# Last batch of a mixture of experts: where the second bias is added, and how the combined sums are turned

## The chip, the cores and the metric

The kernel runs on one core of a Trainium2 chip. The metric is the time of one execution in microseconds, measured on the device; lower is better. The kernel before takes 3936.42 us, the median of three runs (3930.62 to 3939.96).

## What is computed

The input x is 4 images of 384 channels and 32 x 32 points. Layer 0 is a group normalisation, a selective scan over the points in four directions (16 states per channel), a layer norm and a gelu, added to x. Layer 1 takes the points as tokens (4 batches of 1024 tokens of 384 numbers) and adds windowed attention and then a mixture of experts. The change lies in the mixture's end:

```python
scores = jnp.einsum('bsd,de->bse', x, gate_w) + gate_b
probs = jax.nn.softmax(scores, axis=-1)
topk_vals, topk_idx = jax.lax.top_k(probs, TOP_K)          # 2 of 4 experts
mask = jnp.sum(jax.nn.one_hot(topk_idx, NUM_EXPERTS, dtype=probs.dtype), axis=-2)
masked = probs * mask
masked = masked / (jnp.sum(masked, axis=-1, keepdims=True) + 1e-09)
h = jax.nn.gelu(jnp.einsum('bsd,edh->ebsh', x, w1) + b1[:, None, None, :], approximate=False)
y = jnp.einsum('ebsh,ehd->ebsd', h, w2) + b2[:, None, None, :]
out = jnp.einsum('bse,ebsd->bsd', masked, y)
```

All is in 32-bit floats. The bias b2 of an expert is added to each of its outputs, and the two chosen outputs of a token are then weighted with their gates and summed.

## The kernel before

**A recording layer sets the order.** The kernel is written as generators that yield operations. A small planner (`Machine`, lines 218 to 382) keeps a clock for each engine, an assumed cost for each operation and the assumed times at which tiles are written and read, and records on each engine the operation that it holds to be ready first; the numbers EARLY, LATER and the like are handicaps. What is recorded is a fixed program: each engine executes its own list in that order and waits on semaphores. So the order of all later work depends on every assumed time. Buffers come from stocks (`Stock`, line 78): `take` waits until one is free, `give` hands it back together with the later of its assumed writing and reading times (line 113). SP issues all plain DMAs, POOL the indirect ones.

**The scan.** Its 768 steps, in blocks of 128 rows by 1024 points, run over batch after batch. For each step POOL multiplies (`times_b`), ACT makes the decay dA (`decay`), DVE scans, POOL or DVE multiplies by c, and PE folds pairs of steps (`fold_y`). When it has ended (line 879 and on), two more PSUM banks and 15 more row tiles are handed to the other stages: the stock `rows` then has 25.

**Tokens and routes.** When a batch's scan is done, `tokens(b)` runs its 8 tiles of 128 tokens through attention; `route(n)` then sorts half a batch (4 tiles) into blocks of at most 128 tokens of one expert and scatters the tokens' rows into xsdr. A batch has 5 blocks from its first half and 14 from its second, 19 in all and 76 in the kernel.

**A block of an expert.** `loads` (line 1369) reads the block's expert number e and its row rw into registers of SP, and loads b1, the tokens xb and eight pieces of 576 KB of the weights w1 and w2 (w_sb, eight buffers). `turn_in` transposes the tokens, `hidden` makes four groups of nine matmuls (ps_hid), `gelus` the activation, `output` twelve matmuls into one PSUM tile y_ff. `leave` (line 1438) copies y_ff to the one SBUF tile yb and stores it to ysdr. When all 19 blocks of a batch have left, the batch counts as done (line 1447).

**The combination.** `combine(b)` (line 1449) has a generator `one(a)` for each of a batch's 8 tiles. It loads o, the residual, turned (channels on partitions); transposes the gates p of the four experts into a row tile gt (ps_gt); gathers the two expert outputs of each token into gs[0] and gs[1] from ysdr; and weights and sums them, ACT into the PSUM tile ps_c and DVE into gs[0]. Six matmuls into ps_c follow: three with the identity, which turn the sums, and three of b2_sb with gt, which add the gated second bias. DVE adds o, and SP stores the result. For the last batch all 8 tiles run at once and take o and gt early, when their half has been routed; their gathers wait for the batch's last block. The rows gt and gs are given back after the matmuls are recorded (lines 1488 and 1489).

Of the kernel before, what the change touches and what calls it, by code (L numbers as in the profile page):

```python
# [13 lines left out]
ALU = mybir.AluOpType  # L14
# [3 lines left out]
P = 128  # L18
B, D, HH, WW = 4, 384, 32, 32
L = HH * WW  # L20
T = D // P
# [13 lines left out]
NE, HID = 4, 4 * D  # L35
# [357 lines left out]
def conv_attn_hybrid(  # L393
# [11 lines left out]
    def const_load(src, shape, name):  # L405
        dst = const.tile(shape, F32, name=name)
        nc.sync.dma_start(dst, src)
        return dst
# [12 lines left out]
    b2_sb = const_load(b2, [NE, D], "b2_sb")  # L421

    ident = const.tile([P, P], F32, name="ident")
# [64 lines left out]
    banks = Stock(m, ps_b, "ps", 4, [P, HB])  # L488
# [3 lines left out]
    with tc.tile_pool(name="setup", bufs=1) as setup:  # L492
# [16 lines left out]
        for j in range(JB):  # L509
            ps = banks.now("ps_al")  # L510
# [22 lines left out]
    rows = Stock(m, work, "row", NROW, [P, D])  # L533
# [21 lines left out]
    ysdr = [dram.tile([(SPARE + 1) * P, D], F32, name="ysdr", tag=f"ys{n}", bufs=1) for n in range(2)]  # L555
# [16 lines left out]
    pe, act, dve, pool, sp = m.pe, m.act, m.dve, m.pool, m.sp  # L572
# [8 lines left out]
    def copy(dst, src):  # L581

        if on_vector():
            yield from dve.tensor_copy(dst, src)
        else:
            yield from act.copy(dst, src)

    def on_vector():
        lead = FAVOUR if count_of["scan"] < NSLOT else 0.1
        return m.clock["dve"] + lead < m.clock["act"]  # L590
# [768 lines left out]
    rws, bbs, xts, w1s, w2s, hids, left = {}, {}, {}, {}, {}, {}, {}  # L1359

    def turn_in(i, xb):
        xt = yield from xbts.take("xbt")
        ps = yield from three("ps_xb", xb)
        yield from copy(xt[:, :D], ps[:, :D])
        banks.give(ps)
        xts[i] = xt
        xbs.give(xb)

    def loads():
        for i, (n, o) in enumerate(ffn):  # L1370
            yield lambda: n in routed
            xs, idx, p, eid, gate = routed[n]
            e = yield from sp.value_load(eid[0:1, 0, o : o + 1], min_val=0, max_val=NE - 1)
            rw = yield from sp.value_load(eid[0:1, 1, o : o + 1], min_val=0, max_val=SPARE * P)
            rws[i] = rw
            bb = yield from bbs_.take("bb")
            yield from sp.dma_start(bb.unsqueeze(1), b1[:, bass.ds(e, 1), :])
            bbs[i] = bb
            xb = yield from xbs.take("xb")
            yield from sp.dma_start(xb, xs[bass.ds(rw, P), :])  # L1380
            m.spawn(turn_in(i, xb), LATER)
            for store, src in ((w1s, wl1), (w2s, wl2)):
                for c in range(NCH):
                    w = yield from wts.take("w_sb")
                    yield from sp.dma_start(w, src[bass.ds(e, 1), c].rearrange("e p f -> p (e f)"))
                    store[i, c] = w
# [33 lines left out]
    def output():  # L1420
        for i in range(len(ffn)):
            for c in range(NCH):
                yield lambda: (i, c) in hids and (i, c) in w2s
            yield m.settled(*(hids[i, c] for c in range(NCH)))
            y = yield from banks.take("y_ff")
            for c in range(NCH):
                mm = Calls()
                for j in range(HT):
                    mm.matmul(
                        y[:, :D], hids[i, c][:, ts(j, P)], w2s[i, c][:, ts(j, D)],  # L1430
                        start=c == 0 and j == 0, stop=c == NCH - 1 and j == HT - 1,
                    )
                yield from pe.all(mm)
                wts.give(w2s.pop((i, c)))
                hss.give(hids.pop((i, c)))
            m.spawn(leave(i, y), LATER)

    def leave(i, y):
        b = PARTS[ffn[i][0]][0]
        yb = yield from ybs.take("yb")  # L1440
        yield from copy(yb[:, :D], y[:, :D])
        banks.give(y)
        yield from sp.dma_start(ysdr[b % 2][bass.ds(rws.pop(i), P), :], yb[:, :D])
        ybs.give(yb)
        left[b] = left.get(b, 0) + 1
        if left[b] == sum(SIZES):
            have.add(("experts", b))

    def combine(b):

        def one(a):
            n, a_in = 2 * b + a // PT, a % PT
            if b == B - 1:
                yield lambda: n in routed
            xs, idx, p, eid, gate = routed[n]
            if b == B - 1:
                o, gt = yield from rows.take("cb", n=2)
            else:
                o, gt, *gs = yield from rows.take("cb", n=4)
            yield from sp.dma_start(  # L1460
                o[:, :D].rearrange("p (t l) -> p t l", t=T), t2dr[b][:, :, ts(a, P)]
            )
            ps = yield from banks.take("ps_gt")
            yield from pe.transpose(ps[:NE, :P], p[:, a_in, :], ident)
            yield from copy(gt[:NE, :P], ps[:NE, :P])
            banks.give(ps)
            if b == B - 1:
                yield lambda: ("experts", b) in have
                gs = yield from rows.take("cb", n=2)
            for n in range(2):  # L1470
                yield from pool.indirect_dma_start(
                    out=gs[n][:, :D], out_offset=None, in_=ysdr[b % 2],
                    in_offset=bass.IndirectOffsetOnAxis(ap=idx[:, n, a_in : a_in + 1], axis=0),
                )
            yield m.settled(*gs)
            ps = yield from banks.take("ps_c")
            yield from act.activation(ps[:, :D], gs[0][:, :D], AF.Copy, scale=gate[:, 0, a_in : a_in + 1])
            yield from dve.scalar_tensor_tensor(
                gs[0][:, :D], gs[1][:, :D], gate[:, 1, a_in : a_in + 1], ps[:, :D], ALU.mult, ALU.add
            )  # L1480
            mm = Calls()
            for t in range(T):
                c = ts(t, P)
                mm.matmul(ps[:, c], gs[0][:, c], ident, start=t == 0, stop=False)
            for t in range(T):
                c = ts(t, P)
                mm.matmul(ps[:, c], b2_sb[:, c], gt[:NE, :P], start=False, stop=t == T - 1)
            yield from pe.all(mm)
            rows.give(gt, *gs)
            yield from dve.tensor_tensor(o[:, :D], ps[:, :D], o[:, :D], ALU.add)  # L1490
            banks.give(ps)
            yield from sp.dma_start(
                out[b].rearrange("(t p) h w -> p t (h w)", p=P)[:, :, ts(a, P)],
                o[:, :D].rearrange("p (t l) -> p t l", t=T),
            )
            rows.give(o)

        yield from m.together([one(a) for a in range(NT)], 2 if b < B - 1 else NT, LATER)
        have.add(("out", b))

# [16 lines left out]
    with tc.manual_schedule():  # L1517
        for b in range(B):
            m.spawn(group_norm(b), EARLY)
        for gen in (turn_loads(), time_steps(), state_rows(0), state_rows(1), spread(1), spread(0)):  # L1520
            m.spawn(gen, EARLY)
        for gen in (decay(), times_b(), scan()):
            m.spawn(gen)
        m.spawn(layer1(), EARLY)
        m.spawn(routes(), EARLY)
        for gen in (prepare(), loads(), hidden(), output(), mixture()):
            m.spawn(gen, LATER)
        m.run()
# [54 lines left out]
```

## Time and profile before

| what | us |
|---|---|
| median of three runs | 3936.42 |
| the profiled execution | 3933.02 |
| its span, from the first to the last instruction | 3931.3 |
| PE busy | 3031.9 |
| DVE busy | 2911.4 |
| POOL busy | 2879.7 |
| ACT busy | 2441.7 |

The profile is of one execution. "PE" stands for the matmuls of TensorE, "PEld" for its weight loads, DVE for VectorE, ACT for ScalarE, POOL for GpSimd and SP for SyncE, which here only issues DMAs. A line number such as L148 or L159 is that of the planner's helper that issues every operation, so tiles tell the work apart: `ps_c<-ident,cb` writes ps_c from the identity and a row tile. A 32-bit matmul leaves two records, a transpose one. Views used below are the page, the chain of waits that ended last, the timeline (instructions in order of time, equal neighbours merged), groups of instructions, and busy time by stage.

### The profile page before, as it was taken

How to read it: one execution, taken by the hardware profiler on the slowest of the kernel's cores; microseconds unless marked ns; L12 is line 12 of the kernel's file. 1: busy time of each engine (PE TensorE's matmuls, PEld its weight loads, DVE VectorE, ACT ScalarE, POOL GpSimd, SP SyncE). 2: the span in 40 equal slices, each digit the busy share in tenths (PEclk: the TensorE clock that was granted, in tenths of full speed). 3: DMA queues.
4: the chain of work that ended last, by engine and by line, in shares of the span. 5: the costliest groups of instructions: out<-in, count | busy, mean ns of one | idle time of the engine just before them, and what ended most of it. 6: DMA issues, size and time to landing. Idle time of an engine off the chain costs nothing. (4 is left out here: it accounts for less than half of the span.)

```text
span 3931.3 us, 50281 instructions
## 1 busy us (share of the span) xinstructions
PE 3031.9 (77%) x15880; PEld 1853.6 (47%) x15880; DVE 2911.4 (74%) x3331; ACT 2441.7 (62%) x4050; POOL 2879.7 (73%) x1498
## 2 busy tenths in 40 slices
PE   2555555588677898777687769888878999998997
PEld 1100010055444555434354536556545566877786
DVE  2999999988778788898887797877778884332001
ACT  2544454467787788866667858887677775542221
POOL 1999989988888887898898789888887994012001
PEclk8555566577789899977778879988888999998997
DMA  5776775534558998935377769865567997448995
GB/s 205 266 266 208 275 271 185 193 120 153 175 170 306 329 395 303 336 136 170 107 268 259 259 245 374 293 219 176 182 217 268 363 365 235 143 151 298 318 321 184
DMA packets 394147, 953.66 MB, mean 243 GB/s; under 512 B 49621, under 2 KB 173401, under 8 KB 393881
## 3 DMA queue, kind: packets, MB, share of 16 engines
q1 hardware_dynamic: 385688, 925.27, 67.2%
q0 software_dynamic: 8192, 25.17, 1.8%
q8 instruction: 126, 2.06, 0.2%
q14 instruction: 141, 1.15, 0.1%
HBM read 786.39 MB, written 182.78 MB: 247 GB/s over the span
## 5 line engine op out<-in xcount | busy, mean ns | idle before, releaser
L148 POOL TENSOR_TENSOR z<-dts,bc 128x1024 f32<-128x1024 f32 x768 | 1793.4, 2358 | 178.5 <-PE ps_y L159 93.6
L148 ACT ACTIVATE dA<-dts,a 128x1024 f32<-128x1024 f32 x768 | 851.7, 1116 | 473.7 <-DVE z L148 448.8
L159 PE MATMUL ps_y<-z,fold 128*32 128x512 f32 x3072 | 730.6, 771 | 487.7 <-POOL z L148 262.9
L148 POOL TENSOR_TENSOR z<-z,bc 128x1024 f32<-128x1024 f32 x383 | 898.2, 2356 | 139.7 <-DVE z L148 130.0
L148 DVE TENSOR_TENSOR_SCAN dA<-dA,z 128x1024 f32<-128x1024 f32 x385 | 880.6, 2287 | 135.5 <-ACT dA L148 128.5
L148 DVE TENSOR_TENSOR_SCAN z<-dA,z 128x1024 f32<-128x1024 f32 x383 | 862.3, 2276 | 57.0 <-ACT dA L148 54.5
L159 PEld LDWEIGHTS ps_hid<-xbt,w_sb 128*128 128x128 f32 x5472 | 674.4, 200 | 152.8 <-issue 50.7
L159 PE MATMUL ps_hid<-xbt,w_sb 128*128 128x128 f32 x5472 | 698.9, 286 | 48.8 <-DMA w_sb<-wl 13.1
L159 PE MATMUL y_ff<-w_sb,hs 128*128 128x384 f32 x1824 | 659.7, 503 | 28.8 <-ACT hs L148 17.8
L159 PEld LDWEIGHTS ps_y<-z,fold 128*32 128x32 f32 x3072 | 93.8, 120 | 915.3 <-POOL z L148 448.2
L148 DVE TENSOR_TENSOR z<-dA,bc 128x1024 f32<-128x1024 f32 x385 | 470.0, 1221 | 13.2 <-DVE dA L148 0.5
L148 ACT ACTIVATE hs<-ps_hid,bb 128x128 f32<-128x128 f32 x912 | 276.2, 368 | 306.3 <-PE ps_hid L159 255.4
L159 PEld LDWEIGHTS y_ff<-w_sb,hs 128*128 128x128 f32 x1824 | 333.7, 195 | 276.1 <-issue 58.4
L148 POOL DMA_INDIRECT cb<-ysdr,idx x64 | 62.6, 978 | 320.0 <-DMA ysdr<-yb 274.1
L148 ACT ACT_TABLE_LOAD x194 | 248.9, 1283 | 10.3 <-PE ps_g L159 3.6
L304 ACT ACT_TABLE_LOAD x194 | 248.9, 1283 | 4.1 <-PEq L1568 0.8
L159 POOL TENSOR_TENSOR rn<-rn,half 128x1 f32<-128x1 f32 x96 | 52.8, 550 | 212.2 <-DVE rn L159 203.2
L148 DVE COPY yb<-y_ff 128x384 f32<-128x384 f32 x24 | 13.4, 557 | 248.8 <-PE y_ff L159 233.3
L148 ACT ACTIVATE ed<-ps_dt,dtb_sb 128x512 f32<-128x512 f32 x192 | 125.4, 681 | 83.9 <-PE ps_dt L148 78.8
L148 POOL DMA_INDIRECT xsdr<-tks,idx x64 | 65.1, 1016 | 141.8 <-DVE idx L159 56.6
L148 PE MATMUL ps_dt<-xd,dtw_sb 12*128 12x512 f32 x192 | 135.6, 816 | 20.0 <-DMA dtw_sb<-in_dtw_dram 14.7
L148 DVE TENSOR_TENSOR ps_dt<-ps_dt,ed 128x512 f32<-128x512 f32 x192 | 132.7, 691 | 11.7 <-ACT ps_dt L148 8.8
(202 smaller groups left out, 3293.8 us busy)
## 6 DMA issues: line engine op xcount, KB each, us to landing
w_sb<-wl SPq DMA_DIRECT2D x608, 576.0 KB
dts<-dtr SPq DMA_DIRECT2D x384, 512.0 KB
bc<-xdr SPq DMA_DIRECT2D x128, 512.0 KB
dtr<-ed SPq DMA_DIRECT2D x192, 256.0 KB
ub<-udr SPq DMA_DIRECT2D x48, 512.0 KB
yp<-ydr SPq DMA_DIRECT2D x96, 256.0 KB
ydr<-yp SPq DMA_DIRECT2D x96, 256.0 KB
wl<-in_w_dram SPq DMA_DIRECT2D x32, 576.0 KB
```

The lines of the kernel that those rows point to most:

```text
L148: return getattr(self.real, op)(*a, **k)
L159: getattr(self.real, op)(*a, **k)
L304: self.nc.scalar.add_instruction(mybir.InstLoadActFuncSet(name=self.nc.get_next_instruction_name(), act_func_set_id=EXP_LN_SET,))
```

## The change

In the last batch alone, b2 is no longer added in the combination. `leave` loads the row of b2 that belongs to the block's expert into all 128 partitions of yb and adds y_ff to it on DVE, in place of the copy; for this, `loads` keeps the register e beside rw until the block leaves. In the combination of the last batch the row gt, the transpose of the gates and its copy are left out, and the sums are turned by three transposes instead of three matmuls with the identity. In the other batches these operations stay, and the row gt is given back before their six matmuls are recorded and not after.

```diff
             rw = yield from sp.value_load(eid[0:1, 1, o : o + 1], min_val=0, max_val=SPARE * P)
-            rws[i] = rw
+            rws[i] = e, rw
...
     def leave(i, y):
         b = PARTS[ffn[i][0]][0]
+        e, rw = rws.pop(i)
         yb = yield from ybs.take("yb")
-        yield from copy(yb[:, :D], y[:, :D])
+        if b == B - 1:
+            yield from sp.dma_start(
+                yb[:, :D], b2[bass.ds(e, 1), :].to_broadcast([P, D])
+            )
+            yield from dve.tensor_tensor(yb[:, :D], y[:, :D], yb[:, :D], ALU.add)
+        else:
+            yield from copy(yb[:, :D], y[:, :D])
         banks.give(y)
-        yield from sp.dma_start(ysdr[b % 2][bass.ds(rws.pop(i), P), :], yb[:, :D])
+        yield from sp.dma_start(ysdr[b % 2][bass.ds(rw, P), :], yb[:, :D])
...
             if b == B - 1:
-                o, gt = yield from rows.take("cb", n=2)
+                o = yield from rows.take("cb")
             else:
                 o, gt, *gs = yield from rows.take("cb", n=4)
...
-            ps = yield from banks.take("ps_gt")
-            yield from pe.transpose(ps[:NE, :P], p[:, a_in, :], ident)
-            yield from copy(gt[:NE, :P], ps[:NE, :P])
-            banks.give(ps)
-            if b == B - 1:
+            if b < B - 1:
+                ps = yield from banks.take("ps_gt")
+                yield from pe.transpose(ps[:NE, :P], p[:, a_in, :], ident)
+                yield from copy(gt[:NE, :P], ps[:NE, :P])
+                banks.give(ps)
+            else:
                 yield lambda: ("experts", b) in have
                 gs = yield from rows.take("cb", n=2)
...
             mm = Calls()
-            for t in range(T):
-                c = ts(t, P)
-                mm.matmul(ps[:, c], gs[0][:, c], ident, start=t == 0, stop=False)
-            for t in range(T):
-                c = ts(t, P)
-                mm.matmul(ps[:, c], b2_sb[:, c], gt[:NE, :P], start=False, stop=t == T - 1)
+            if b < B - 1:
+                for t in range(T):
+                    c = ts(t, P)
+                    mm.matmul(ps[:, c], gs[0][:, c], ident, start=t == 0, stop=False)
+                for t in range(T):
+                    c = ts(t, P)
+                    mm.matmul(ps[:, c], b2_sb[:, c], gt[:NE, :P], start=False, stop=t == T - 1)
+                rows.give(gt)
+            else:
+                for t in range(T):
+                    mm.transpose(ps[:, ts(t, P)], gs[0][:, ts(t, P)], ident)
             yield from pe.all(mm)
-            rows.give(gt, *gs)
+            rows.give(*gs)
```

## The prediction

> **What bounds the kernel now.** I read the page's busy table and its 40 slices, then the chain of waits, then the end in the timeline, and last the busy time by stage.
>
> ```profile
> PE 3031.9 (77%) x15880; PEld 1853.6 (47%) x15880; DVE 2911.4 (74%) x3331; ACT 2441.7 (62%) x4050; POOL 2879.7 (73%) x1498
> PE   2555555588677898777687769888878999998997
> DVE  2999999988778788898887797877778884332001
> POOL 1999989988888887898898789888887994012001
> ```
>
> Until slice 33 POOL and DVE, which carry the scan, are the fullest rows; from there PE stands at 9 and the other two fall. The last scan instruction starts at 3276 us. So there are a scan stretch and, from about 3280, one in which PE works off what is left of the mixture of experts.
>
> ```profile
> 3100.00:3200.00 100.00, 96.29 (x573) 63.62 (x573) 86.76 (x56) 73.53 (x111) 96.70 (x46) 0.99 1.02 392
> 3200.00:3300.00 100.00, 96.70 (x603) 66.91 (x602) 73.17 (x46) 72.38 (x111) 75.68 (x33) 1.00 0.86 294
> 3674.00:3690.00 16.00, 16.00 (x100) 12.93 (x99) 0.56 (x1) 3.90 (x13) 0.00 (x0) 1.00 0.94 317
> 3886.00:3932.00 46.00, 25.41 (x96) 21.63 (x96) 8.94 (x17) 4.67 (x8) 15.19 (x16) 0.54 0.37 107
> ```
>
> The columns are PE, PEld, DVE, ACT, POOL, granted clock, DMA share, GB/s. PE is already full in the last 180 us of scan; in the steady blocks of the last batch it has no gap (a block takes 16.1 us, the distance of two evictions of y_ff); at the end its clock is down to 0.54.
>
> ```profile
> 3895.73 3.04 DMA cb<-ysdr,idx
> 3899.56 12.70 PE ps_c L159 x48
> 3913.41 6.39 PE ps_c L159 x24
> 3921.05 6.36 PE ps_c L159 x24
> 3927.44 0.56 DVE cb L148
> ```
>
> The chain's end: after one gather has landed, eight tiles of ps_c on PE follow one another, 3.15 us each (two groups of three, below).
>
> ```profile
> 3888.77 0.99 POOL L148 DMA_INDIRECT cb<-ysdr,idx  x1 [274.05 <-DMA ysdr<-yb]
> 3891.96 0.97 POOL L148 DMA_INDIRECT cb<-ysdr,idx  x1 [2.20 <-issue]
> ...
> 3910.61 0.95 POOL L148 DMA_INDIRECT cb<-ysdr,idx  x1 [0.30 <-issue]
> ...
> 3924.18 1.65 PE L159 MATMUL ps_c<-ident,cb 128*128 128x128 f32 x6
> 3925.75 1.65 PE L159 MATMUL ps_c<-cb,b_sb 4*128 4x128 f32 x6
> ```
>
> The 16 gathers leave POOL every 1.25 us, the last at 3910.6; without PE's queue the end would stand some 4 us after that.
>
> ```profile
> 3609.62 0.99 POOL L148 DMA_INDIRECT xsdr<-tks,idx  x1 [1.94 <-DMA xsdr<-tks,idx]
> 3609.81 5.29 SPq L148 DMA_DIRECT2D cb<-t2dr  x8
> 3621.72 0.88 PE L159 MATMUL ps_xb<-ident,xb 128*128 128x128 f32 x3 [6.69 <-DMA xb<-xsdr]
> ```
>
> A hole before the last 14 blocks: the load of xb waits for the scatters of the last route, and PE has run out of blocks. The evictions before and after it are at 3604.6 and 3648.4: 43.8 us for one block (16.1), two tiles of ps_c (3.5 warm) and eight ps_gt (2.2), so some 22 us are lost here.
>
> **The Trainium skill.** "TensorE: Matmul & The Clock Gate", Part 1, says that PE runs at half clock after an idle window and needs some 3.4 us of work to warm; Part 4 that transposes do not count as such work, so the tail will stay cold. The trace agrees with the first: three transposes of ps_xb last 0.49 us warm and 0.88 after the hole. "ScalarE: Activation LUTs", What ACT_TABLE_LOAD costs, gives 1283 ns a load; here the mean is 1283. "DMA: Bandwidth & Descriptors", Anatomy of one DMA, gives some 2 us fixed cost; the last store is issued at 3886.1 and the gather that waits for it starts at 3888.8.
>
> **The change part by part.**
>
> *The tail.* Per tile, two groups of three matmuls (3.15 us) become three transposes (0.88). DVE then needs 0.61 + 0.56 a tile, which is less than the 1.25 of a gather. With one row for each tile instead of two, 8 + 16 rows fit into 25 (10, and 15 that the scan gives back), so no gather waits for a row; before, two did (0.32 and 0.82 us over the usual 0.30). All gathers leave by 3891.96 + 14 x 1.253 = 3909.5; the last lands 3.0 later, at 3912.5; DVE 0.6, PE 0.9, DVE 0.6 and hops 0.2 end at 3914.8. Before it was 3928.0. **-13.2 us**. Bounds: -14 (warm transposes), -10 (each transpose at the 0.476 us maximum of its row, and a late gather).
>
> *The bias.* Nineteen evictions become additions on DVE, 0.56 us each from PSUM as in the row cb<-ps_c, against 0.56 for the copy. DVE is nearly empty there: nothing. Each has a new load of one row of b2 into 128 partitions, 192 KB, like xb; 0.62 us of transfer at the 317 GB/s of a steady block. In the built order it stands on SP between bb and xb, behind the store of the block before. That store is issued at 3827.98, bb of the next block at 3839.32: its landing is long past, so SP doesn't stand. The load has until 3843.5, when y is full: 3.6 us, enough for 2 plus 0.6. Queued behind it are xb and eight w_sb; the first w_sb is issued at 3840.4 and needed at 3847.4. A delay of 0.6 (an issue and its DMA) fits into those 7 us. Cover gone, it would be 19 x 0.62 = 12 us at most; DMA share rises from 0.93 to 0.965. I take **0**, ends 0 and +12. The last block's load waits for the store issued at 3876.3, is in by 3881, and y is ready at 3885.4: nothing.
>
> *The eight ps_gt of the last batch* go, 8 x 0.27: **-2.2**.
>
> *What is moved.* In batches 0 to 2 the row gt is given back before its matmuls are recorded rather than after. Costs are the same, but the recording layer now fills its queues otherwise: the two built orders agree up to the first combination (scan instruction 416 of 768, 1735 us) and differ from there on all engines. I counted the built orders. At scan 704 (3044 us) half a block less has been done than before; at the end of scan 49 of 76 blocks instead of 51. Behind the scan stand 72 more matmuls of ps_hid (8 groups of nine, 2.0 us each), 21 more of y_ff (7 groups of three, 1.95) and six transposes: 16.0 + 13.7 + 0.7 = **+30.3**.
>
> Some comes back. In the hole, the last route now comes with 57 blocks done rather than 59, and two whole blocks (31.6) and four tiles of ps_c (7) stand between it and the first load of xb that must wait for its scatters; from route to xb it was 46 us before, with ten gathers among the scatters, and six now. 39 us of work nearly cover it: **-20** of 22 (ends 0 and -22).
>
> And between scan 704 and the end PE has 1.5 blocks less (24 us) in a stretch where it was 96% busy. This stretch took 238 us. Its second half went at 3.35 us a scan instruction, about POOL's own work (2.36 x 45/32 = 3.32), its first at 4.02; 64 x 3.35 = 214. So the gain lies between 0 and -23; with the end of a token tile moved into it I take **-10**.
>
> ACT has 404 table loads instead of 388: ten in scan, six behind. 16 x 1.283 = 20.5; against ten stand 24 gelus fewer (24 x 0.368 = 8.8), so scan's net is 12.8 - 8.8 = **+4**; those behind lie on an ACT that is half idle, 0. Ends 0 and +20.
>
> From scan 416 to 704 both orders do nearly the same work otherwise mixed: 1309 us, 4.55 us a scan instruction, where the undisturbed start has 3.3 to 3.7. A view doesn't give the sign; 1.5% either way is 20 us. I take 0, ends -20 and +20.
>
> Sum: -13.2 - 2.2 + 30.3 - 20 - 10 + 4 = **-11**. The profiled execution took 3933.0 (span 3931.3 and 1.7 around it), 3.4 below the median; 3936.4 - 11 = **3925**.
>
> **Rivals.**
>
> *The two blocks are not repaid* (slower). Place: the end of scan. If POOL and DVE, not PE, set the pace to the end, scan ends no earlier, and 30.3 are added. With the hole closed only by half (-10) and the tail (-15.4) that is +5; with the sixteen table loads in ACT's way, the scan waiting for dA, +20.5 more: about +15 to +25, 3954. It decides if scan ends less than 5 us earlier and the hole keeps half its length. For it: DVE waits for ACT's dA in many of its gaps; against it: PE's 96%.
>
> *The new mixture in the middle is better* by some 20 us on top: 3905. For it: batch 1's blocks are done eight scan instructions earlier. Against: more table loads.
>
> *The b2 loads collide* with the weights: at DMA share 0.93, +10 of the 12: 3935, no change. Against: PE hasn't one wait on w_sb in the steady blocks.
>
> That the change doesn't do what it says is out: the built order has 24 products of ps_c in the end for 48.
>
> **How the numbers follow.** Forecast 0.42, own range 3908 to 3934; not repaid 0.36; better middle 0.12; collision 0.10. A measurement of this kernel tells 0.2%, 7.9 us. Faster: 0.34 of the forecast and 0.12 = 0.46. Same: 0.08 + 0.03 + 0.08 = 0.19. Slower: 0.33 + 0.02 = 0.35. The range takes in the better middle and most of the first rival: 3898 to 3966.
>
> **What would show it.** Tail: from the last y_ff to the end 32 to 33 us rather than 46, chain on POOL's gathers. Steady blocks at 16.1 us; a longer block means a collision. No gap on xb near the last route. Last scan instruction 5 to 15 us before 3276; if it is later, the middle has lost and I am wrong, whatever the tail does.

## The result, and the profile after

The changed kernel takes 3968.0 us (median of 6 runs, 3956.2 to 3973.3); before took 3940.7 in 6 runs of its own, three of them beside it. The ratio is 1.0071, 95% interval 1.0056 to 1.0087: slower by some 28 us. The forecast was 3925.

The profiled execution took 3970.0, its span is 3968.3 us, 37.0 longer than before's. The page of the changed kernel:

```profile
PE 3034.0 (76%) x15800; PEld 1845.0 (46%) x15800; DVE 2912.9 (73%) x3337; ACT 2461.0 (62%) x4050; POOL 2875.8 (72%) x1496
...
L148 DVE TENSOR_TENSOR yb<-y_ff,yb 128x384 f32<-128x384 f32 x19 | 10.6, 555 | 242.8 <-DMA yb<-in_b_dram 150.2
```

No engine has over 3 us more work than before (PE 3031.9, DVE 2911.4), except ACT with its further table loads (19 us). The second row is new: before the additions of b2 DVE stands mostly for their own load. Where the copies stood before, it was for y_ff:

```profile
L148 DVE COPY yb<-y_ff 128x384 f32<-128x384 f32 x24 | 13.4, 557 | 248.8 <-PE y_ff L159 233.3
```

The tail, from the timeline of the changed kernel:

```profile
3958.22 0.94 POOL L148 DMA_INDIRECT cb<-ysdr,idx  x1 [0.31 <-issue]
3958.53 0.55 DVE L148 TENSOR_TENSOR cb<-ps_c,cb 128x384 f32<-128x384 f32 x1
3958.66 0.90 PE L159 MATMUL ps_c<-ident,cb 128*128 128x128 f32 x3 [0.73 <-DVE cb L148]
...
3964.60 0.56 DVE L148 TENSOR_TENSOR cb<-ps_c,cb 128x384 f32<-128x384 f32 x1 [0.43 <-PE ps_c L159]
```

PE now has gaps and follows the gathers; the last addition ends 7 us after the last gather starts, where before it was 17.4. From the last eviction of y_ff to the end of the span it is 33.5 us instead of 45.3. So the tail did about what was forecast, and the loss lies before it. Read from the timelines of the two kernels:

| stretch | before, us | after, us | difference |
|---|---|---|---|
| start to last scan instruction | 3276.4 | 3271.8 | -4.6 |
| to the last route's indices | 306.8 | 313.8 | +7.0 |
| to the ps_hid of the first block that had to wait for that route's scatters | 41.4 | 58.4 | +17.0 |
| from there to the last eviction of y_ff | 261.4 (16 blocks) | 290.9 (17 blocks) | +29.5 |
| tail | 45.3 | 33.5 | -11.8 |

The pair makes 37 us of the 28: the profiled execution of before was 7.7 us faster than its median, that of the changed kernel 2.0 slower. It shows in the first row. Up to the last scan instruction six runs below (x1, x3, x4, x6, x10, x11) have the same instructions in the same order as before, and three (x2, x5, x7) the same as the changed kernel. In the seven profiles of the old order that instruction starts at 3276.4 to 3292.7, on the mean at 3283.4; in the four of the new order at 3263.9 to 3271.8, on the mean at 3267.6. So the scan ends some 16 us earlier, not 4.6.

The hole before the last blocks, and a stand of PE ahead of it, in the changed kernel's timeline:

```profile
3483.00 0.90 PE L159 MATMUL ps_x<-ident,yl 128*128 128x128 f32 x3 [8.04 <-ACT yl L148]
...
3586.32 10.15 PE L159 MATMUL ps_hid<-xbt,w_sb 128*128 128x128 f32 x72 [7.42 <-DVE xbt L148]
...
3594.74 1.00 POOL L148 DMA_INDIRECT xsdr<-tks,idx  x1 [0.30 <-issue]
...
3601.96 1.00 POOL L148 DMA_INDIRECT xsdr<-tks,idx  x1 [3.69 <-DMA xsdr<-tks,idx]
...
3628.57 1.65 PE L159 MATMUL ps_c<-ident,cb 128*128 128x128 f32 x6 [5.69 <-DVE cb L148]
...
3629.28 1.00 POOL L148 DMA_INDIRECT xsdr<-tks,idx  x1 [0.59 <-DMA xsdr<-tks,idx]
...
3633.37 0.35 SPq L148 DMA_DIRECT2D xb<-xsdr  x1
...
3643.95 8.30 PE L159 MATMUL ps_hid<-xbt,w_sb 128*128 128x128 f32 x72 [0.54 <-DVE xbt L148]
```

The eight scatters of the last route run from 3594.7 to 3630.3, mostly each waiting until the one before it has landed; then comes the load of xb, and only at 3643.95 the block. From the route's indices to that block PE was busy for 48.2 us of 58.1 and idle for 9.9; before, for 29.1 of 41.2, idle for 12.1. Before, its longest stand there was for xb (6.69 us, shown with the prediction). In the changed kernel it doesn't stand for xb at all; its two long stands, 3.15 and 5.69 us, are in front of tiles of ps_c of batch 2. From the last scan instruction to the indices PE was idle for 30.2 us, before for 12.5: two stands of 8.04 us (at 3475) and 7.42 us (at 3579) are new. x2 and x5, in the new order, have both; none of the seven profiles of the old order, nor x9, has a stand of over 3 us there.

And a steady block of the last batch, and below it one of before:

```profile
3752.82 0.33 SPq L148 DMA_DIRECT2D yb<-in_b_dram  x1
3753.35 0.33 SPq L148 DMA_DIRECT2D xb<-xsdr  x1
...
3758.18 0.56 DVE L148 TENSOR_TENSOR yb<-y_ff,yb 128x384 f32<-128x384 f32 x1 [16.17 <-DMA yb<-in_b_dram]
...
3759.01 0.52 PE L159 MATMUL ps_xb<-ident,xb 128*128 128x128 f32 x3 [0.62 <-DMA xb<-xsdr]
```

```profile
3839.86 0.33 SPq L148 DMA_DIRECT2D xb<-xsdr  x1
...
3845.31 0.49 PE L159 MATMUL ps_xb<-ident,xb 128*128 128x128 f32 x3
```

PE waits 0.62 us for xb, which it had not done before. A block has 16.65 us on the mean of eleven, before 16.14.

### The profile page after: what moved, and what is told of

Same layout as the page of the kernel before. It is cut to its first block, busy times and chain, and to the rows that moved or that the text cites. A ratio compares the mean times of both kernels' runs of the same rounds, so it can differ in the third digit from the quotient of the medians.

```text
span 3968.3 us, 50187 instructions
## 1 busy us (share of the span) xinstructions
PE 3034.0 (76%) x15800; PEld 1845.0 (46%) x15800; DVE 2912.9 (73%) x3337; ACT 2461.0 (62%) x4050; POOL 2875.8 (72%) x1496
## 4 chain that ended last, share of the span: by engine, by line
PE 35%; ACT 12%; DVE 9%; DMA 7%; issue 5%; POOL 5%; SPq 1%; POOLq 0%; DVEq 0%; ACTq 0%
PE y_ff L159 10%; PE ps_hid L159 9%; PE ps_y L159 4%; POOL z L148 4%; DVE dA L148 3%; ACT dA L148 2%; DVE z L148 2%; ACT L304 2%; PE ps_qk L159 2%; ACT L148 2%; PE ps_o L159 2%; DMA xb<-xsdr 2%; PE ps_pr L159 2%; DMA w_sb<-wl 2%; SPq L148 1%
## 5 line engine op out<-in xcount | busy, mean ns | idle before, releaser
L159 PE MATMUL y_ff<-w_sb,hs 128*128 128x384 f32 x1824 | 670.1, 509 | 25.3 <-ACT hs L148 17.7
L148 DVE TENSOR_TENSOR z<-dA,bc 128x1024 f32<-128x1024 f32 x387 | 472.3, 1220 | 12.8 <-DVE dA L148 0.5
L148 ACT ACT_TABLE_LOAD x202 | 259.2, 1283 | 11.8 <-PE ps_g L159 5.1
L148 DVE TENSOR_TENSOR yb<-y_ff,yb 128x384 f32<-128x384 f32 x19 | 10.6, 555 | 242.8 <-DMA yb<-in_b_dram 150.2
```

The lines of the kernel that those rows point to most:

```text
L148: return getattr(self.real, op)(*a, **k)
L159: getattr(self.real, op)(*a, **k)
```

## The experiments

All ratios are to the kernel before, run beside them; 0.1% is 3.9 us. Two theories stood at the start: A, the loss is the order that the moved `give` makes; B, it is the last batch's own new operations.

**x1: the line moved back.**

```diff
-                rows.give(gt)
             else:
                 for t in range(T):
                     mm.transpose(ps[:, ts(t, P)], gs[0][:, ts(t, P)], ident)
             yield from pe.all(mm)
+            if b < B - 1:
+                rows.give(gt)
             rows.give(*gs)
```

> The changed kernel with one line moved back: the row gt of batches 0 to 2 is given back after its matmuls are recorded, as before. The recorded order then equals that of before up to the routes of the last batch (51 blocks done at the end of scan, 388 table loads). Theory A (the loss is the order that the moved line makes): tail -12, eight ps_gt -2, b2 loads in the last blocks +9, so about 5 us under before: 3930 to 3940, and over 25 us under the changed kernel. Theory B (the loss comes from the last batch's own new operations): about as the changed kernel, 3960 to 3970.

Measured: ratio 0.9999 (0.9988 to 1.0011). The 28 us are gone.

**x2: the moved line alone, in the kernel before.**

```diff
+            if b < B - 1:
+                rows.give(gt)
             yield from pe.all(mm)
-            rows.give(gt, *gs)
+            if b == B - 1:
+                rows.give(gt)
+            rows.give(*gs)
```

> Before with the moved line alone: gt of batches 0 to 2 is given back before its matmuls are recorded, the last batch is as before. The order up to the end of scan is that of the changed kernel (49 blocks done, 404 table loads). Theory A: +25 to +40 us over before, 3965 to 3980, with the last scan instruction near 3272 us as in both profiles and the first block of the last route's half later by some 30 us than before; the chain's end 45 us after the last block as before. Theory B: within 8 us of before.

Measured: 1.0072 (1.0056 to 1.0089), 28 us. The moved line alone costs what the whole change costs, and by x1 the rest of it nets nothing. Theory B falls. In x2's profile the last scan instruction starts at 3263.9, the first block that waits for the last scatters is the 60th, as in the changed kernel, and has its ps_hid 58.4 us after the route's indices, and the tail is 44.0. That block comes 9 us later than before, not some 30; the rest of the loss lies in the further block behind it. From the last scan instruction to the last eviction PE was busy for 612.8 us (before 584.3) and idle for some 39 (before 25).

**x3: b2 loaded among the weights.** On x1:

```diff
                     store[i, c] = w
+                if store is w1s and PARTS[n][0] == B - 1:
+                    bt = yield from rows.take("b2r")
+                    yield from sp.dma_start(bt[:, :D], b2[bass.ds(e, 1), :].to_broadcast([P, D]))
+                    b2s[i] = bt
...
-            yield from sp.dma_start(
-                yb[:, :D], b2[bass.ds(e, 1), :].to_broadcast([P, D])
-            )
-            yield from dve.tensor_tensor(yb[:, :D], y[:, :D], yb[:, :D], ALU.add)
+            bt = b2s.pop(i)
+            yield from dve.tensor_tensor(yb[:, :D], y[:, :D], bt[:, :D], ALU.add)
+            rows.give(bt)
```

> x1 with the row of b2 loaded into a row tile of its own between the w1 and the w2 weights of its block, not into yb just ahead of the next xb; the same bytes. If the last blocks are longer because the b2 load stands ahead of xb on SP's queue (place), a block is 16.1 us again and the time is 9 us under x1, 3922 to 3930. If they are longer because the DMA engines have 192 KB more to move (bandwidth), a block stays at 16.6 to 16.8 and the time equals x1 within 4 us.

**x4: no b2 load in the last batch.** On x1:

```diff
-            yield from sp.dma_start(
-                yb[:, :D], b2[bass.ds(e, 1), :].to_broadcast([P, D])
-            )
-            yield from dve.tensor_tensor(yb[:, :D], y[:, :D], yb[:, :D], ALU.add)
+            yield from dve.tensor_copy(yb[:, :D], y[:, :D])
```

> x1 without the load of b2 and its addition in the last batch: y_ff is copied on DVE. The second bias of the last batch is left out. A block is 16.1 us; 8 to 11 us under x1, about 14 us under before (tail -12, ps_gt -2): 3922 to 3928. If it equals x1, the b2 load costs nothing and the longer blocks of the changed kernel have another cause.

Measured: x3 0.9968 (0.9949 to 0.9986), x4 0.9966 (0.9950 to 0.9981): 12 to 13 us under before and under x1 by these ratios, 9 to 12 by the medians. A block is 16.13 us in both, 16.56 in x1. So the same 192 KB are free behind xb and cost some 9 to 13 us just ahead of it. The profiles show some 6 of these: from the first waiting block to the last eviction x1 takes 267 us, x3 and x4 261, and all gaps of PE from 0.1 us up in x1's blocks are waits for xb (8, 4.4 us in all). Busy time by stage, the changed kernel above and x3 below (PE, PEld, DVE, ACT, POOL, clock, DMA share, GB/s):

```profile
3757.00:3774.00 17.00, 16.38 (x102) 13.04 (x101) 0.56 (x1) 4.02 (x13) 0.00 (x0) 1.00 0.92 317
```

```profile
3740.00:3756.00 16.00, 16.00 (x100) 12.82 (x99) 0.56 (x1) 3.91 (x13) 0.00 (x0) 1.00 0.96 333
```

x3 moves more per microsecond and PE has no gap; the changed kernel has gaps at a lower rate of transfer. So it wasn't bandwidth that ran out.

**x5 and x6: batch 2's combination after the last route.** On the changed kernel (x5) and on x3 (x6):

```diff
             yield lambda: ("experts", b) in have or (b == B - 1 and 2 * b + 1 in routed)
+            if b == B - 2:
+                yield lambda: 2 * B - 1 in routed
```

> The changed kernel, with the combination of batch 2 started only when the last route has been recorded: its gathers no longer stand among the last route's scatters on POOL, nor its ps_c ahead of blocks on PE. Theory C (the hole before the last blocks stays open in the changed kernel because those gathers delay the scatters and ps_c holds PE's queue, so that the two further blocks are not hidden in it): scatters end within 26 us of the route's indices instead of 44, the hole loses 15 to 20 us, 3948 to 3955. Theory D (the two blocks cost their 16 us each whatever stands there, the hole is set by the scatters' own chain): within 5 us of the changed kernel, 3963 to 3973.

> The same edit on x3 (gt given back as before, b2 loaded among the weights). Theory C: the hole of 22 us is cut by 6 to 12 us, 3920 to 3926, which would be the shortest of all. Theory D: as x3, 3928 to 3935.

Measured: x5 1.0063 (1.0050 to 1.0077), as the changed kernel; x6 1.0005 (0.9996 to 1.0014), some 15 us over x3 by the ratios, a loss that neither theory forecast. With no gathers among them the scatters of x5 still took 33 us:

```profile
3590.67 1.03 POOL L148 DMA_INDIRECT xsdr<-tks,idx  x1 [26.75 <-DMA xb<-xsdr]
3595.53 0.96 POOL L148 DMA_INDIRECT xsdr<-tks,idx  x1 [3.83 <-DMA xsdr<-tks,idx]
3601.49 0.96 POOL L148 DMA_INDIRECT xsdr<-tks,idx  x1 [5.00 <-DMA xsdr<-tks,idx]
...
3623.17 0.96 POOL L148 DMA_INDIRECT xsdr<-tks,idx  x1 [1.88 <-DMA xsdr<-tks,idx]
```

Each waits for the landing of the one before it; POOL's own time is 1 us of 4.6. The first, by the record, also waits for a load of xb to have read xsdr. So the first half of theory C falls: without the gathers the chain is 2 us shorter than the changed kernel's 35 (in x6 28 us, in x3 31), not 15 to 20.

Its second half, ps_c in PE's way, was not tested, for the edit left tiles of ps_c ahead of the waiting block on PE, and their gathers now came after the scatters. The longest stands of PE in the two holes, x5 above and x6 below:

```profile
3631.90 1.65 PE L159 MATMUL ps_c<-ident,cb 128*128 128x128 f32 x6 [12.17 <-DVE cb L148]
```

```profile
3628.19 1.65 PE L159 MATMUL ps_c<-ident,cb 128*128 128x128 f32 x6 [26.65 <-DVE cb L148]
...
3634.50 0.90 PE L159 MATMUL ps_xb<-ident,xb 128*128 128x128 f32 x3
```

In x6 xb had been issued at 3619.10, and PE turned it only after two tiles of ps_c. The hole between two evictions grew to 58.3 us (3601.9 to 3660.2; in x3 38.3), and the stretch behind it by 9.7 us, as six of batch 2's eight tiles of ps_c (1.76 us each warm) now lie there; in x3 four lay between the indices and the waiting block and four before. In x5 the same move neither cost nor won anything that can be measured; its hole ended 4.5 us sooner, and the rest isn't resolved. What the hole would be with no ps_c in it wasn't run.

**x7: copies of xbt on ACT once the scan has ended.** On the changed kernel:

```diff
-        yield from copy(xt[:, :D], ps[:, :D])
+        yield from (act.copy if ended else copy)(xt[:, :D], ps[:, :D])
```

> The changed kernel, with the copies of ps_xb to xbt put on ACT once the scan has ended. In the changed kernel's profile PE stands 7.4 us at 3579 for a copy of xbt that is queued on DVE behind the whole calculation of the last route. If that stand is on the path, 5 to 8 us less than the changed kernel: 3960 to 3963. If the wait for the last scatters absorbs it (PE runs out of blocks before xb arrives in any case), within 3 us of the changed kernel.

Measured: 1.0067 (1.0054 to 1.0080), within the interval of the changed kernel. In x7's timeline that stand of 7.4 us is down to 0.57, but PE stands longer in front of ps_c later (4.23, 3.16 and 3.58 us), and the waiting block still starts 58 us after the indices. So this stand by itself isn't visibly on the path.

**x9: gt given back early in batch 1 alone.** The same edit as x2, with `b == 1` for `b < B - 1`.

> Before, with gt given back early in batch 1 alone. The order is that of before up to the first combination of batch 1 (scan instruction 650 or so), and 1.5 blocks less have been done at the end of scan (49.75 instead of 51.25; x2 has 49.25), with 402 table loads. If the loss of x2 is the blocks that slip behind the scan, 16 us each, less what scan ends earlier: +14 to +24 us over before. If it is the other mixture in scan instructions 416 to 650: within 8 us of before.

Measured: 1.0053 (1.0040 to 1.0065), 21 us. Until instruction 640 of the scan the timeline keeps within 5 us of that of before (there 2734.0 against 2734.7), so the mixture in the middle is not needed for the loss. 1.5 blocks behind the scan went with 21 us, 2 blocks in x2 with 28: 14 us each, a little under the 16.1 of a block. In x9 the scatters start as soon as the indices are there, as before; PE's idle time from there to the waiting block is 12.8 us all the same. That is two points of one kind; an order that brings more blocks before the scan's end wasn't tried.

**x10: matmuls with the identity instead of the transposes.** On x3:

```diff
-                    mm.transpose(ps[:, ts(t, P)], gs[0][:, ts(t, P)], ident)
+                    mm.matmul(ps[:, ts(t, P)], gs[0][:, ts(t, P)], ident, start=True, stop=True)
```

> x3 with the last batch's sums turned by three matmuls with the identity, as before, instead of three transposes. If the tail now runs at the pace of POOL's gathers (1.25 us each), PE's 1.6 us a tile in place of 0.9 shows only behind the last gather and where two tiles come close together: tail 1 to 3 us longer than x3's 34.3, so the time within 5 us of x3. If the transposes are what shortened the tail, it is 8 x 0.7 = 6 us longer or more.

Measured: 0.9954 (0.9937 to 0.9972), the lowest of all, though its interval overlaps that of x3; the tail is 33.5 us against x3's 34.3. The transposes bring nothing. Most of the 16 us by which x10's profiled execution is shorter than x3's lies before the last route's indices, where the two run the same program, so the matmuls aren't shown to be the faster form either. x10's timeline:

```profile
3904.90 6.11 PE L159 MATMUL ps_c<-ident,cb 128*128 128x128 f32 x30 [19.07 <-DVE cb L148]
...
3911.56 0.94 PE L159 MATMUL ps_c<-ident,cb 128*128 128x128 f32 x6 [0.55 <-DVE cb L148]
...
3915.29 0.91 PE L159 MATMUL ps_c<-ident,cb 128*128 128x128 f32 x6 [0.90 <-DVE cb L148]
```

The first five tiles run together, and then three matmuls take 0.91 us, as much as three transposes in the changed kernel's tail (0.90): the matmuls have warmed PE, the transposes have not. The granted clock (last column but two) says the same, x10 above and the changed kernel below:

```profile
3911.50:3919.90 8.40, 2.75 (x18) 2.23 (x18) 3.66 (x8) 0.00 (x0) 0.00 (x0) 0.98 0.66 193
```

```profile
3950.00:3968.00 18.00, 7.16 (x24) 4.02 (x24) 8.74 (x16) 1.17 (x2) 7.04 (x8) 0.50 0.64 184
```

**x11: b2 loaded twice.** On x3:

```diff
                     yield from sp.dma_start(bt[:, :D], b2[bass.ds(e, 1), :].to_broadcast([P, D]))
+                    b3 = yield from rows.take("b2x")
+                    yield from sp.dma_start(b3[:, :D], b2[bass.ds(e, 1), :].to_broadcast([P, D]))
+                    rows.give(b3)
```

> x3 with the same row of b2 loaded a second time, into another row tile that nobody reads, just behind the first load: 384 KB more in a block than before. If bytes are free as long as they stand behind xb (place decides), a block stays at 16.1 us and the time is within 4 us of x3. If the DMA engines were already near their end with one load (share 0.93 before), a block grows by 0.3 us or more, at least 5 us over x3.

Measured: 0.9988 (0.9976 to 0.9999), and the block stays at 16.12 us:

```profile
3700.00:3716.00 16.00, 16.00 (x100) 12.88 (x99) 0.56 (x1) 3.82 (x13) 0.00 (x0) 1.00 1.01 354
3740.00:3756.00 16.00, 16.00 (x100) 12.84 (x99) 0.56 (x1) 3.79 (x14) 0.00 (x0) 1.00 0.95 347
```

In the steady blocks even twice the bytes are free, at 347 to 354 GB/s; in one block close behind the hole PE waited 2.85 us for xb (x3 0.39). The time is some 8 us over x3's by the ratios, more than the 4 that were forecast, but the two intervals overlap. Of the 6.4 us between the two profiled executions 6.0 lie before the last scan instruction, where the order is the same; whether the second load costs anything as a whole is open.

## Why the prediction was wrong

The forecast of the last batch held but for the load of b2; the account of the moved order did not, and that decided. For the moved line alone the forecast came to +4 us (30.3 - 20 - 10 + 4); x2 measured +28. The likely case was given 0.42, "the two blocks are not repaid" 0.36 at 3954. This rival is the nearest to what happened, 14 us above its price and at 3968 just outside the range, but its reason, a scan that ends no sooner, isn't what the profiles of the same order show.

*The tail*, -13.2: -11.8 by the profile. Right, with the cause half right: the b2 products and the queue behind them were the cost, not the form of the turning (x10). PE's 0.9 a tile with transposes is the cold rate, as expected.

*The bias*, 0 with an end at +12: 10 us by the medians of x1 and x4, some 6 of them seen in the profiles. The load was priced at 2 plus 0.6 us, with w_sb as the waiting load and 7 us to spare. It was xb. In the block shown xb was issued behind b2 and by the chain of waits landed 5.5 us later, and before PE wanted it 5.3 us after its issue (3839.86 to 3845.2); b2's own row, issued at 3752.82, let the addition start at 3758.18. "The b2 loads collide" was right in size but put it on the DMA share; it is the place in SP's queue (x3).

*Behind the scan*, +30.3: this term was right. From the last scan instruction to the last eviction PE had 31.3 us more work in the changed kernel and 28.5 in x2.

*The hole*, -20: this is the step that failed. Its words were "39 us of work nearly cover it". The work came, two blocks in the window and 48.2 us of PE; the idle time did not go. From the indices to the waiting block PE was idle for 12.1 us before, 9.9 in the changed kernel and 11.1 in x2, while the window grew from 41.2 us to 58. Two things were wrong. The 22 us to be won were too many: PE's gaps between the two evictions sum to 11.8, and between them lay one and a half blocks of ps_hid, not one, in part at the cold rate. (Behind the hole stand 16 blocks, not 14.) And in the new order the stands are in front of ps_c and not of xb, so work that is listed behind ps_c can't fill them. The scatters also started 9 us after the indices instead of at once: on POOL two gathers of batch 2 stood ahead of them, and a load of xb had still to read xsdr (in x5, without these gathers, it was 6 us). From the first start to the last they took 34.5 us instead of 30.1, but 30 to 33 in the other runs of the old order with the same combination. How the longer window divides between the start of the chain and ps_c wasn't separated.

*A term that the forecast lacked*: PE's idle time between the last scan instruction and the last route's indices, taken at nothing, was 30.2 us instead of 12.5 (27.0 in x2). Two stands of some 8 and 7.4 us are most of it.

*Scan*, -10: the sign held, the working did not. In the mean of the profiles scan ended 16 us earlier. But the 1.5 blocks fewer did not speed up scan instructions 704 to 767: these took 246 to 249 us in the four profiles of the new order and 231 to 235 in the seven of the old. In that stretch now stood the route of batch 2's second half (its indices at 3078, before 3020); instructions 712 to 720 took 50.5 us instead of 33.6. The middle, instructions 416 to 704, taken at 0 with ends of 20, took 1282 to 1285 us instead of 1309 to 1318, a gain beyond its end; why isn't known. That the two together have the sign of the forecast is luck.

*Table loads*, +4: not seen apart; x9 has 402 of them, x2 404, and the difference of these two in time goes with the blocks as well.

For x2 the terms behind the scan are 28.5 us of work and 13.5 of idle time; less 16 of scan that is 26, against the 28 measured. That the blocks slip and where PE then stands is read from the profiles; that the moved line is the cause is what x1 and x2 show.

## What to carry to other kernels

Where an order is made by assumed times, a line that changes only when a buffer counts as free can cost more than the operations that it was moved for: run it alone first. Price a gap by the engine's own idle time in it, not by the distance of two events, and ask what stands first in the engine's list there: work that is listed behind the waiting instruction doesn't fill its wait. A difference of some us between two single profiles can lie in a stretch where both have the same order: compare all profiles that share it. A new load is priced by the first load queued behind it and by that one's slack, not by its bytes. Of the versions run here x10 has the lowest time, 0.9954 of before: the bias added at the eviction, b2's row loaded among the weights, `give` where it was, matmuls with the identity. x3, with transposes, isn't told apart from it.

## What the runs showed of the hardware

Three 32-bit matmuls of 128 x 128 took as long warm (0.91 us, x10's tail) as three transposes did cold (0.90, the changed kernel's tail); the granted clock was 0.98 in the one and 0.50 in the other. "TensorE: Matmul & The Clock Gate", Part 4, says that transposes do not count as work for the clock; x10 against the changed kernel agrees, but doesn't prove it, since x10's first five tiles ran for 6.1 us in one piece and the transposes stood in bursts with gaps of 0.3 to 1.4 us.

At a DMA share of 0.92 a load of 192 KB landed 5.5 us after its issue (xb at 3753.35), more than twice the 2 us that "DMA: Bandwidth & Descriptors", Anatomy of one DMA, gives as fixed cost; that section is on DMAs issued by POOL, and this one is issued by SP. PE felt a load of equal size ahead of it. At 0.95 to 1.01 (x11) it did not in the steady blocks, with the load in another place.

Eight scatters that wait for one another took 27 to 37 us from the first start to the last in the twelve kernels, 3.8 to 5.3 us from one to the next, of which POOL's own time is 1.0.
